# Padding the ragged weights of layer 3's last run to 128 by 128, and turning layer 1's column numbers from a 128-wide buffer

## The chip, the core and the metric

The kernel runs on one core of a Trainium2 chip. The number that counts is the device time of one execution in microseconds (us). A core has five engines, each with an instruction stream of its own that it works off in order: PE multiplies matrices (a load of the stationary operand, PEld, and then a matmul that streams the moving operand), DVE does elementwise work and reductions, ACT applies functions, POOL is a general engine for elementwise work, and SP only starts transfers here. They meet through semaphores alone: an instruction that waits holds up everything behind it on its engine.

## The reference, cut to what matters

Four graph layers over one dense 2708 x 2708 adjacency matrix that is mostly zero, with 128 features. Each layer is `x = x + layer(relu(layernorm(x)), adj)`:

```python
# layer 0: a weighted mean over the graph
x = x + (adj.T @ h) / adj.sum(axis=0)[:, None]
# layer 1: a message for every edge, then an update
messages = gelu(s[:, None, :] + d[None, :, :] + msg_b)
aggregated = einsum('ijd,ij->id', messages, adj)
...
# layer 2: agg = adj @ h, then a gated recurrent cell
# layer 3: graph attention with two heads
for i in range(2):
    e = leaky_relu(s_src[:, None] + s_dst[None, :])
    e = where((adj > 0) | eye(n), e, NEG)
    att = layernorm(softmax(e, axis=1) @ h_i + x)
    h_next = h_next + elu(att @ ff1_w[i].T) / 2
```

What matters for the change is layer 3's product `softmax(e) @ h_i`, and in layer 1 the list of column numbers of the nonzero entries. Numbers are fp32, but for small integers and split values, which are bf16.

## The kernel before

2708 rows are 21 tiles of 128 (`P`) and one of 20 (`TAIL`), so `NT` is 22; `size(t)` is the height of tile t, `span(t, k)` the first column and the number of columns of k tiles, here up to the end of the matrix. The last tile is ragged wherever it appears: as 20 rows of a stationary operand (its contraction), or as 20 columns of it.

**Layer 3, weights.** Each nonzero of the attention matrix is, up to factors that cancel, `max(row, lift) * mask`: a row of numbers that is the same for all partitions, a number for each partition, and the 0/1 mask as uint8. `weigh(run, unit, pool)` (L923) makes a tile `wt` of these on DVE in one instruction. A *run* is a group of consecutive target tiles, and `RUNS = ((0, 3), (3, 8), (11, 8), (19, 3))`: the last one holds tiles 19, 20 and the ragged 21, so it is 276 columns wide. A *unit* is one source tile j and one head k, 44 of them to a run.

**Layer 3, products.** `products` (L955) walks over the units. It asks for the weights of unit u, and then multiplies with those of unit u - 3 (u - 2 in the first run): for each of the run's target tiles q, 128 columns of `wt` are the stationary operand and `hv[:, j, k, :]`, 129 wide (128 features and the sum of weights), is the moving one. As the operands are fp32, one such product stands in the trace as two loads and two matmuls. In the last run the third target tile has 20 columns; in the last two units of every run `wt` and `hv` have 20 rows. A pool `l3w` of five buffers holds the weights, so DVE can be at most five units ahead of PE.

**What goes on beside.** The results of a run gather in PSUM banks. `evacuate` copies them out to `res` at the start of the next run (on ACT and DVE), and `close` then turns two target tiles at a time into output: scaling and a layer norm on DVE (L1018, L118 to L131, with a power on POOL, L121), a rescale on ACT (L137), transposes (L1029) and a product (L1038) on PE, an exponential linear unit on ACT and POOL, two sums on DVE (L1055, L1056) and a store. These steps are put between the products by a clock counted in estimated us (`spend`, `advance`, `follow`): the order on each engine is written out by hand (`tc.manual_schedule()`), and no engine reorders it. The last run's results are read straight from PSUM (`in_place`).

**Layer 1.** For each row tile t, `place` makes on DVE the list of the nonzero values and of their column numbers (`where`, 128 x 22 bf16, one column for each block of 124 matrix columns). `pass_on(t)` (L552) transposes `where` on PE, copies it out on ACT, stores it to DRAM and loads it back broadcast to all partitions; `columns` makes one-hot matrices from it. PE's main work here is `combine` (L612, L616) and `gather` (L637). `period(t)` puts the steps of one tile in order by hand; there are 22 tiles.

**Layer 2 and what it leaves.** `aggregate` loads pieces of the transposed matrix (`a`, five source tiles by 512 columns, three buffers) on SP's queue, writes `mask` from them, four fifths on DVE (L1086) and one fifth on POOL (L1089), and multiplies (L1094). A buffer is free for the next load when DVE, POOL and PE have all read it. Layer 3's lasting tiles (`hv`, `lift`, `row`, `score`, `mask`) are made just ahead of layer 2, in space that layer 1 has left; `score`'s last tile is set to zero there on POOL (L887), since its rows 20 to 127 are read later.

Of the kernel before, what the change touches and what calls it, by code (L numbers as in the profile page):

```python
# [20 lines left out]
F32 = mybir.dt.float32  # L21
BF16 = mybir.dt.bfloat16
AF = mybir.ActivationFunctionType
ALU = mybir.AluOpType
AX = mybir.AxisListType
# [5 lines left out]
P = 128  # L31
N = 2708
D = 128
NT = (N + P - 1) // P
# [10 lines left out]
NB = (N + JB - 1) // JB  # L45
S = 8
E = P
# [4 lines left out]
def size(t):  # L52
    return min(P, N - t * P)
# [7 lines left out]
def listed_layers(ctx: ExitStack, tc: tile.TileContext, x, adj, w, out, flag):  # L61
    nc = tc.nc
# [84 lines left out]
    def span(t, k):  # L147

        return t * P, min(k * P, N - t * P)
# [29 lines left out]
    ident_h = keep.tile([P, P], BF16, name="ident_h")  # L179
# [25 lines left out]
    with tc.tile_pool(name="l0c", bufs=1) as fix:  # L205
# [33 lines left out]
        with (  # L239
# [76 lines left out]
            with tc.manual_schedule():  # L316
# [4 lines left out]
                for gi, (g0, gk) in enumerate(GROUPS):  # L321
# [11 lines left out]
                    for j in range(NT):  # L333
# [6 lines left out]
                        n = g0 + j // 5  # L340
# [54 lines left out]
    with (  # L395
# [25 lines left out]
            nc.gpsimd.tensor_tensor(dst[2], rest, dst[1], ALU.subtract)  # L421

        state = {}

        def count_rows(t):
            some = work.tile([P, NB, S], BF16, name="some")
            nc.vector.tensor_scalar(some, val[:, t, :, :], 0.0, None, ALU.is_gt)
            with nc.allow_low_precision("counts up to 8"):
                nc.vector.reduce_sum(rows_n[:, t, :], some, AX.X)

        def compare(dst, numbers, op):

            nc.vector.tensor_tensor(  # L433
                dst.rearrange("p b (x r) -> p b x r", r=R),
                count_h.rearrange("p (x r) -> p x r", r=R).unsqueeze(1).to_broadcast([P, NB, P // R, R]),
                numbers.unsqueeze(2).to_broadcast([P, NB, P // R, R]),
                op,
            )
# [60 lines left out]
        def place(t):  # L499

            st = state[t]
            lead = st["lead"]
            slot = work.tile([P, NB], F32, name="slot")
            nc.vector.tensor_scalar(slot, lead[:, :, R], part, -1.0, ALU.subtract, ALU.mult)
            hot = once.tile([P, NB, S], F32, name="hot")
            nc.vector.tensor_tensor(
                hot,
                count[:, 0:S].unsqueeze(1).to_broadcast([P, NB, S]),
                slot.unsqueeze(2).to_broadcast([P, NB, S]),
                ALU.is_equal,  # L510
            )
            picked = once.tile([P, NB, 4, S], F32, name="picked")
            for half, y in enumerate(st.pop("ys")):
                bs = slice(half * HB, (half + 1) * HB)
                nc.vector.tensor_tensor(
                    picked[:, bs, :, :],
                    y[:, :, 0 : 4 * S].rearrange("p b (q s) -> p b q s", s=S),
                    hot[:, bs, :].unsqueeze(2).to_broadcast([P, HB, 4, S]),
                    ALU.mult,
                )  # L520
            value = work.tile([P, NB], F32, name="value")
            where = work.tile([P, NB], BF16, name="where")
            with nc.allow_low_precision("column numbers"):
                nc.vector.tensor_reduce(where, picked[:, :, 3, :], AX.X, ALU.max)
            nc.vector.reduce_sum(value, picked[:, :, 0:3, :], AX.XY)
            mine = work.tile([P, NB, P], BF16, name="mine")
            compare(mine, lead[:, :, 0:R], ALU.is_equal)
            st["value"], st["where"], st["mine"] = value, where, mine
# [19 lines left out]
        def pass_on(t):  # L548

            st = state[t]  # L550
            p = rpool.tile([P, 2 * CH], BF16, tag="r", name="p_w")
            nc.tensor.transpose(p[0:NB, 0:E], st.pop("where"), ident_h)  # L552
            turned = work.tile([NB, E], BF16, name="where_T")
            nc.scalar.copy(turned, p[0:NB, 0:E])
            passed = wdram.tile([NB, E], BF16, name="passed")
            nc.sync.dma_start(passed, turned)
            st["spread"] = once.tile([P, NB, E], BF16, name="spread")
            nc.sync.dma_start(
                st["spread"].rearrange("p b e -> p (b e)"), passed.rearrange("b e -> (b e)").partition_broadcast(P)
            )  # L560
# [148 lines left out]
        def period(t, between=()):  # L709
# [5 lines left out]
            for k in range(GB):  # L715
# [32 lines left out]
                if k == 3 and b:  # L748
                    place(t + 2)
# [132 lines left out]
    mask = l3.tile([P, NT, N], U8, name="mask")  # L882
    hv = l3.tile([P, NT, 2, D + 1], F32, name="hv")
    lift = l3.tile([P, NT, 2], F32, name="lift")
    row = l3.tile([P, 2, N], F32, name="row")
    score = l3.tile([P, NT, 4], F32, name="score")
    nc.gpsimd.memset(score[:, NT - 1, :], 0.0)  # L887
    ident_8 = l3.tile([P, P], U8, name="ident_8")
    nc.vector.tensor_copy(ident_8, ident)
    PIECE = 5  # L890
    RUNS = ((0, 3), (3, 8), (11, 8), (19, 3))
    MOST = 8
# [9 lines left out]
    def spend(units):  # L902
        clock[0] += units

    def advance():

        for f in list(following):
            while f[1] <= clock[0]:
                wait = next(f[0], None)
                if wait is None:  # L910
                    following.remove(f)
                    break
                f[1] = clock[0] + wait

    ready = set()

    def weigh(run, unit, pool):

        c, n = span(*run)
        j, k = divmod(unit, 2)  # L920
        kj = size(j)
        wt = pool.tile([P, n], F32, name="wt")
        nc.vector.scalar_tensor_tensor(  # L923
            wt[0:kj, :], row[0:kj, k, c : c + n], lift[0:kj, j, k : k + 1], mask[0:kj, j, c : c + n],
            op0=ALU.max, op1=ALU.mult,
        )
        return wt

    def products(run, numbers, pool, ahead, before=None):

        banks = None
        wts = []
        units = 2 * NT
        touched = set()
        for u in range(units + ahead):
            if u < units:
                while u // 2 not in ready:
                    spend(0.5)
                    advance()
                wts.append(weigh(run, u, pool))  # L940
            v = u - ahead
            if v < 0:
                continue
            if v == 0:
                if before:
                    before()
                banks = banks_of(run, numbers)
            r0, rn = run
            j, k = divmod(v, 2)
            kj = size(j)  # L950
            wt = wts[v]
            for q in range(rn):
                m = size(r0 + q)
                s = k * rn + q
                nc.tensor.matmul(  # L955
                    banks[s // 3][0:m, s % 3, :], wt[0:kj, q * P : q * P + m], hv[0:kj, j, k, :],
                    start=(v < 2 and s // 3 not in touched), stop=(j == NT - 1), skip_group_check=True,
                )
                touched.add(s // 3)
            spend(0.29 * rn)  # L960
            advance()
        return banks

    def banks_of(run, numbers):
        return [
            accs.tile([P, CH], F32, tag=f"acc{b}", name="att")[:, 0 : 3 * (D + 1)].rearrange("p (s d) -> p s d", s=3)
            for b in numbers[0 : (2 * run[1] + 2) // 3]
        ]
# [15 lines left out]
    def evacuate(run, banks):  # L984

        r0, rn = run
        res = out_pool.tile([P, 2 * MOST, D + 1], F32, name="res")
        inv3 = out_pool.tile([P, 2 * MOST], F32, name="inv3")
        tails = (rn - 1, 2 * rn - 1) if size(r0 + rn - 1) < P else ()
        for s in tails:  # L990
            nc.gpsimd.memset(res[:, s, :], 1.0)
        s = 0
        while s < 2 * rn:
            k = min(3 - s % 3, 2 * rn - s)
            m = P
            if s in tails:
                k, m = 1, TAIL
            elif s + k - 1 in tails:
                k -= 1
            copy = nc.vector.tensor_copy if s // 3 % 3 == 2 else nc.scalar.copy  # L1000
            copy(res[0:m, s : s + k, :], banks[s // 3][0:m, s % 3 : s % 3 + k, :])
            s += k
        nc.vector.reciprocal(inv3[:, 0 : 2 * rn], res[:, 0 : 2 * rn, D])
        return [res[:, s, :] for s in range(2 * rn)], inv3, True
# [64 lines left out]
    with (  # L1069
# [140 lines left out]
        for g, (t0, k0) in enumerate(GROUPS):  # L1210
# [6 lines left out]
            advance()  # L1217
        last = RUNS[0]
        banks = products(last, (0, 1), vpool, 2)

    out_pool = ctx.enter_context(tc.tile_pool(name="l3o", bufs=2))
# [5 lines left out]
    over = out_pool.tile([P, 1], F32, name="over3")  # L1227
    nc.vector.reduce_sum(over, wide, AX.XY)
    nc.vector.tensor_tensor(flag, flag, over, ALU.add)

    with tc.tile_pool(name="l3w", bufs=5) as wpool, tc.manual_schedule():
        for run, numbers in zip(RUNS[1:], ((2, 3, 4, 5, 0, 1), (2, 3, 4, 5, 0, 1), (2, 3))):
# [4 lines left out]
            banks = products(run, numbers, wpool, 3, work_off)  # L1237
# [467 lines left out]
```

## Time and profile before

| | us |
|---|---|
| median of 3 runs (1072.81 to 1073.6) | 1073.51 |
| span of the profiled execution, first to last instruction | 1069.6 |
| what lies around it, against the median | 3.9 |

| engine | busy, us | share of the span |
|---|---|---|
| PE, matmuls | 950.0 | 89% |
| DVE | 824.4 | 77% |
| PE, weight loads | 754.1 | 71% |
| ACT | 515.4 | 48% |
| POOL | 398.7 | 37% |

The stages follow each other: layer 0 to about 240 us, layer 1 to 615 us, layer 2 to about 785 us, layer 3's runs to 1047 us (the last run's products begin at 998 us), and the closing of the last run to the end. Of the page, the part on slices shows this as rows of 40 digits: PE is at 9 in nearly all slices of layers 1 to 3 and drops to 3 in the last one.

A line of a group of instructions reads: source line, engine, operation, output<-inputs, shapes (partitions x elements), count | busy us, mean ns of one | idle time of the engine ahead of them and what ended it. For PE `128*20` means 128 rows and 20 columns of weights. A line of a timeline reads: start, duration, the same, and in brackets the idle time ahead of it. Matmuls overlap: what counts is from start to start of one to the next, not their duration.

### The profile page before, as it was taken

How to read it: one execution, taken by the hardware profiler on the slowest of the kernel's cores; microseconds unless marked ns; L12 is line 12 of the kernel's file. 1: busy time of each engine (PE TensorE's matmuls, PEld its weight loads, DVE VectorE, ACT ScalarE, POOL GpSimd, SP SyncE). 2: the span in 40 equal slices, each digit the busy share in tenths (PEclk: the TensorE clock that was granted, in tenths of full speed). 3: DMA queues.
4: the chain of work that ended last, by engine and by line, in shares of the span. 5: the costliest groups of instructions: out<-in, count | busy, mean ns of one | idle time of the engine just before them, and what ended most of it. 6: DMA issues, size and time to landing. Idle time of an engine off the chain costs nothing. (4 is left out here: it accounts for less than half of the span.)

```text
span 1069.6 us, 21992 instructions
## 1 busy us (share of the span) xinstructions
PE 950.0 (89%) x7950; PEld 754.1 (71%) x7950; DVE 824.4 (77%) x2853; ACT 515.4 (48%) x1428; POOL 398.7 (37%) x476
## 2 busy tenths in 40 slices
PE   5798889934799999999999979999978999999993
PEld 2454445433799999899899934444578999999772
DVE  7999999768577798787878265666578977997673
ACT  7777777634766666666666522433321200320142
POOL 3311112022776656666766163343410300430132
PEclk9999999766799999999999979999989999999996
DMA  9888996221233433322221075566300000000000
GB/s 365 315 303 316 316 342 243 78 65 46 88 109 106 124 95 106 106 91 83 97 96 57 28 256 186 185 225 216 91 22 26 9 1 1 6 15 1 2 15 14
DMA packets 60625, 129.67 MB, mean 121 GB/s; under 512 B 11160, under 2 KB 23828, under 8 KB 57798
## 3 DMA queue, kind: packets, MB, share of 16 engines
q1 hardware_dynamic: 58690, 125.38, 34.2%
q10 hardware_dynamic: 1816, 2.80, 0.8%
q8 instruction: 64, 1.05, 0.4%
q14 instruction: 55, 0.45, 0.1%
HBM read 81.55 MB, written 30.87 MB: 105 GB/s over the span
## 5 line engine op out<-in xcount | busy, mean ns | idle before, releaser
L955 PE MATMUL att<-hv,wt 128*128 128x129 f32 (+2 forms) x1936 | 243.8, 283 | 8.7 <-DVE wt L923 8.7
L955 PEld LDWEIGHTS att<-hv,wt 128*128 128x128 f32 (+2 forms) x1936 | 224.7, 192 | 25.8 <-DVE wt L923 10.1
L923 DVE SCALAR_TENSOR_TENSOR wt<-row,lift,mask 128x1024 f32<-128x1024 f32 (+5 forms) x176 | 160.3, 939 | 34.9 <-PE att L955 34.8
L536 POOL TENSOR_SCALAR put<-mine,value 128x128 f32<-128x128 bf16 x176 | 149.8, 867 | 70.3 <-DVE mine L433 67.9
L612 PE MATMUL p_m<-s,sel 128*128 128x128 bf16 x1452 | 161.6, 220 | 5.4 <-ACT g L624 5.4
L616 PE MATMUL p_m<-d,cols 124*128 124x128 bf16 (+1 forms) x1452 | 161.7, 220 | 1.4 <-DVE cols L566 1.3
L121 POOL TENSOR_TENSOR n_r<-n_r,minus_half 128x4 f32<-128x4 f32 (+1 forms) x31 | 46.1, 1486 | 286.5 <-DVE n_r L120 280.9
L637 PE MATMUL agg<-put,g 128*128 128x128 f32 (+1 forms) x968 | 135.9, 281 | 0.0
L297 PE MATMUL acc<-a,hs 128*128 128x512 f32 (+2 forms) x264 | 124.4, 574 | 10.8 <-ACT hs L137 10.8
L309 PEld LDWEIGHTS p_T<-ident,a 128*128 128x128 f32 x484 | 60.1, 144 | 88.3 <-issue 40.3
L637 PEld LDWEIGHTS agg<-put,g 128*128 128x128 f32 x968 | 118.2, 192 | 0.0
L1094 PE MATMUL p_agg<-a,hs 128*128 128x512 f32 (+2 forms) x264 | 109.3, 556 | 7.3 <-DMA a<-adjT 7.2
L612 PEld LDWEIGHTS <-sel 128*128 128x128 bf16 x1452 | 104.3, 98 | 10.8 <-issue 7.0
L285 DVE FIND_INDEX8 col<-val,a 128x8 uint16<-128x124 f32 (+1 forms) x400 | 108.1, 285 | 0.0
L309 PE MATMUL p_T<-ident,a 128*128 128x128 f32 x484 | 82.3, 289 | 26.2 <-ACT aT L313 19.4
L624 ACT ACTIVATE g<-p_m 128x512 f32<-128x512 f32 x132 | 73.1, 554 | 63.8 <-PE p_m L616 63.8
L616 PEld LDWEIGHTS <-cols 124*128 124x128 bf16 (+1 forms) x1452 | 102.5, 98 | 1.9 <-DVE cols L566 1.9
L544 ACT ACTIVATE put<-mine,value 128x128 f32<-128x128 bf16 x308 | 100.5, 391 | 0.0
L283 DVE MAX8 val<-a 128x8 f32<-128x124 f32 (+1 forms) x400 | 92.8, 276 | 2.5 <-DMA a<-in_adj 2.5
L313 ACT ACTIVATE aT<-p_T 128x512 f32<-128x512 f32 (+2 forms) x132 | 71.1, 541 | 47.9 <-ACT aT L313 32.7
L1094 PEld LDWEIGHTS p_agg<-a,hs 128*128 128x128 f32 (+1 forms) x264 | 47.5, 194 | 55.8 <-issue 54.2
L297 PEld LDWEIGHTS acc<-a,hs 128*128 128x128 f32 (+1 forms) x264 | 44.7, 202 | 25.9 <-issue 14.8
(252 smaller groups left out, 1418.7 us busy)
## 6 DMA issues: line engine op xcount, KB each, us to landing
a<-in_adj SPq DMA_DIRECT2D x21, 1354.0 KB
adjT<-aT SPq DMA_DIRECT2D x105, 256.0 KB
a<-adjT SPq DMA_DIRECT2D x20, 1280.0 KB
spread<-passed SPq DMA_DIRECT2D x22, 704.0 KB
later<-sel SPq DMA_DIRECT2D x22, 616.0 KB
row<-own_d ACTq DMA_DIRECT2D x10, 256.0 KB
later<-sel SPq DMA_DIRECT2D x22, 82.5 KB
adjT<-aT SPq DMA_DIRECT2D x21, 74.0 KB
```

The costliest lines, as they stand in the source:

```text
L283: nc.vector.max(val[:, n, b, :], block(b))
L285: nc.vector.max_index(col[:, n, b, :], val[:, n, b, :], block(b))
L297: nc.tensor.matmul(accs[ci][:, 0:cw], h[0:m, n, :], sets[n // 4][0:m, n % 4, c : c + cw], start=(n == 0), stop=(n == NT - 1),)
L309: nc.tensor.transpose(p[0:k, q * P : q * P + m], sets[gi][0:m, q, j * P : j * P + k], ident[0:m, 0:m])
L536: nc.gpsimd.tensor_scalar(st["put", 0][:, b, :], st["mine"][:, b, :], st["value"][:, b : b + 1], None, ALU.mult)
L544: nc.scalar.activation(st["put", 1][:, b - HP, :], st["mine"][:, b, :], AF.Identity, scale=st["value"][:, b : b + 1])
L612: nc.tensor.matmul(p[:, b - b0, :], st["sel"][:, b, :], s3[:, q, t % 2, :], start=(q == 0), stop=False)
L616: nc.tensor.matmul(p[:, b - b0, :], st["cols"][0:kb, b, :], d3[0:kb, b, q, :], start=False, stop=(q == 2))
L637: nc.tensor.matmul(agg, g[:, b - 4 * k, :], put, start=(b == 0), stop=False)
L923: nc.vector.scalar_tensor_tensor(wt[0:kj, :], row[0:kj, k, c : c + n], lift[0:kj, j, k : k + 1], mask[0:kj, j, c : c + n], op0=ALU.max, op ...
L955: nc.tensor.matmul(banks[s // 3][0:m, s % 3, :], wt[0:kj, q * P : q * P + m], hv[0:kj, j, k, :], start=(v < 2 and s // 3 not in touched), ...
L1094: nc.tensor.matmul(pa[:, 0:n], h[0:k, j, :], a[0:k, j - j0, 0:n], start=(j == 0), stop=(j == NT - 1))
```

## The change

Layer 3's last run writes its weights to five buffers of its own, `padded`, 384 columns wide, which are set to zero once ahead of the second run; columns 276 to 383 stay zero. All products of all runs then take 128 columns and 128 rows of weights and write 128 rows of PSUM. For the ragged source tile the last tiles of `hv`, `lift` and `mask` are set to zero on POOL ahead of layer 2, so rows 20 to 127 of the weights and of `hv` are zero. `res` has one buffer instead of two. In layer 1, `where` becomes one of two lasting 128 x 128 buffers (set to zero once), of which the first 22 columns are written and all 128 are transposed.

```diff
         state = {}
+        wheres = [fix.tile([P, P], BF16, name=f"where{q}") for q in range(2)]
+        for q in range(2):
+            nc.gpsimd.memset(wheres[q], 0.0)
...
-            where = work.tile([P, NB], BF16, name="where")
+            where = wheres[t % 2]
             with nc.allow_low_precision("column numbers"):
-                nc.vector.tensor_reduce(where, picked[:, :, 3, :], AX.X, ALU.max)
+                nc.vector.tensor_reduce(where[:, 0:NB], picked[:, :, 3, :], AX.X, ALU.max)
...
-            nc.tensor.transpose(p[0:NB, 0:E], st.pop("where"), ident_h)
+            nc.tensor.transpose(p[:, 0:E], st.pop("where"), ident_h)
...
     nc.gpsimd.memset(score[:, NT - 1, :], 0.0)
+    nc.gpsimd.memset(hv[:, NT - 1, :, :], 0.0)
+    nc.gpsimd.memset(lift[:, NT - 1, :], 0.0)
+    nc.gpsimd.memset(mask[:, NT - 1, :], 0)
...
+    padded = []
+
     def weigh(run, unit, pool):
 
         c, n = span(*run)
         j, k = divmod(unit, 2)
-        kj = size(j)
-        wt = pool.tile([P, n], F32, name="wt")
+        wt = pool.tile([P, n], F32, name="wt") if n == run[1] * P else padded[unit % len(padded)]
         nc.vector.scalar_tensor_tensor(
-            wt[0:kj, :], row[0:kj, k, c : c + n], lift[0:kj, j, k : k + 1], mask[0:kj, j, c : c + n],
+            wt[:, 0:n], row[:, k, c : c + n], lift[:, j, k : k + 1], mask[:, j, c : c + n],
             op0=ALU.max, op1=ALU.mult,
         )
         return wt
...
             j, k = divmod(v, 2)
-            kj = size(j)
             wt = wts[v]
             for q in range(rn):
-                m = size(r0 + q)
                 s = k * rn + q
                 nc.tensor.matmul(
-                    banks[s // 3][0:m, s % 3, :], wt[0:kj, q * P : q * P + m], hv[0:kj, j, k, :],
+                    banks[s // 3][:, s % 3, :], wt[:, q * P : (q + 1) * P], hv[:, j, k, :],
                     start=(v < 2 and s // 3 not in touched), stop=(j == NT - 1), skip_group_check=True,
                 )
...
-        res = out_pool.tile([P, 2 * MOST, D + 1], F32, name="res")
+        res = out_pool.tile([P, 2 * MOST, D + 1], F32, bufs=1, name="res")
...
+
+    for q in range(5):
+        padded.append(out_pool.tile([P, RUNS[-1][1] * P], F32, tag=f"padded{q}", bufs=1, name=f"padded{q}"))
+        nc.gpsimd.memset(padded[q], 0.0)
```

## The prediction, made before the changed kernel was run

> **What bounds the kernel now.** I read the page's slices first: PE is at 9 tenths through layers 1 to 3, DVE between 7 and 9, DMA idle after layer 2. The chain that ended last holds only the last microsecond, so it carries nothing; stages have to be read one by one. Next the busy times of two stretches, one in the middle of an eight-tile run and one in the last run (columns: length, then busy time and count of PE, PEld, DVE, ACT, POOL, granted clock, DMA):
>
> ```profile
> 960.00:980.00 20.00, 20.00 (x182) 20.00 (x181) 14.70 (x13) 0.00 (x0) 0.00 (x0) 1.00 0.00 1
> 1003.00:1009.00 6.00, 6.00 (x38) 3.98 (x38) 3.72 (x12) 1.65 (x4) 0.00 (x0) 1.00 0.00 1
> ```
>
> PE is full in both, at the same clock, but in the first it starts a matmul every 0.110 us (20/182), in the second every 0.158. The timeline of weight loads shows why (three units of the last run):
>
> ```profile
> 1003.99 0.76 PEld L955 LDWEIGHTS att<-hv,wt 128*128 128x128 f32 x6 [0.21 <-issue]
> 1004.96 0.76 PEld L955 LDWEIGHTS att<-hv,wt 128*128 128x128 f32 x6 [0.21 <-issue]
> 1005.93 0.76 PEld L955 LDWEIGHTS att<-hv,wt 128*128 128x128 f32 x6 [0.21 <-DVE n_r L128]
> ```
>
> A unit of six matmuls takes 0.97 us; six at the other rate would take 0.66. The 0.21 of idle on the load side recurs at every return to full width. To the nanosecond, the matmul starts within a unit are 0.11 apart between full ones, but 0.205 into the 20-column pair, 0.124 within it and 0.204 out of it. So crossing from one shape of weights to another costs about 0.09 each way. The same stands in layer 1 (PE's timeline):
>
> ```profile
> 337.01 0.72 PE L637 MATMUL agg<-put,g 128*128 128x128 f32 x5
> 337.67 0.23 PE L552 MATMUL p_w<-ident_h,where 128*22 128x128 bf16 x1
> 337.82 0.34 PE L612 MATMUL p_m<-s,sel 128*128 128x128 bf16 x3
> ```
>
> The last L637 starts at 337.46 and L552 0.205 later, where L637 to a full-width L612 elsewhere takes 0.111; L552 to L612 is 0.157, where L612 to L612 takes 0.056. Now DVE in the last run, by groups over 999 to 1042:
>
> ```profile
> L923 DVE SCALAR_TENSOR_TENSOR wt<-row,lift,mask 128x276 f32<-128x276 f32 x37 | 18.4, 526 | 5.4 <-PE att L955 5.4
> L923 DVE SCALAR_TENSOR_TENSOR wt<-row,lift,mask 20x276 f32<-20x276 f32 x2 | 1.0, 497 | 1.0 <-PE att L955 1.0
> ```
>
> PE sets the pace there, but DVE waits for it only 6.4 us in 43. That is the next bound. Then the entry to layer 2, where the change adds work on POOL:
>
> ```profile
> 629.37 0.10 POOL L887 MEMSET score<- 128x4 f32 x1 [0.57 <-DVE xs L694]
> 629.45 7.15 POOL L1089 TENSOR_SCALAR mask<-a 128x512 uint8<-128x512 f32 x3
> ...
> 632.02 3.48 SPq L1082 DMA_DIRECT2D a<-adjT  x2
> ...
> 637.86 1.10 PE L1094 MATMUL p_agg<-a,hs 128*128 128x512 f32 x2 [1.11 <-DMA a<-adjT]
> ```
>
> The first of POOL's three masks ends at 631.99 and SP issues the fourth load at 632.02; PE runs dry and waits 1.11 us for that load. This path has no slack. Last, the granted clock around the 20-row units that end a run (they start at 903.7 and 993.9):
>
> ```profile
> 902.83:906.24 3.41, 3.41 (x31) 3.29 (x30) 2.21 (x3) 0.96 (x2) 0.00 (x0) 1.00 0.02 5
> 906.24:909.65 3.41, 3.41 (x17) 3.18 (x16) 2.21 (x5) 0.96 (x2) 0.00 (x0) 0.50 0.00 0
> 994.99:998.40 3.41, 3.41 (x30) 3.17 (x29) 1.50 (x5) 1.81 (x4) 0.00 (x0) 1.00 0.02 5
> 998.40:1001.81 3.41, 3.41 (x13) 2.16 (x14) 3.24 (x16) 0.00 (x0) 0.11 (x1) 0.50 0.00 0
> ```
>
> After each such stretch the clock is halved, though PE was never idle.
>
> **What the skill says.** "TensorEngine Tiling (Array Packing)", Key Properties: changing the tiling mode drains the engine. The trace agrees, with 0.09 us each way, and a return to 128 columns costs as much as leaving it. "TensorE: Matmul & The Clock Gate", What's actually happening: the clock is halved by default and freed by activity, judged in windows of some 3.4 us. The trace's steps are 3.41 us, and here a window filled with 20-row matmuls counted as inactive. "VectorE: DVE Perf Modes", Zero memsets can be issued as uint32: a memset takes one cycle per element whatever the type. POOL's two large ones agree (2359 ns for 2708 fp32, 2444 for 2816 bf16: 0.87 ns each); no uint8 one is in the trace. "SBUF — State Buffer", Who interferes with whom: DVE in a two-port mode and POOL lock each other out. POOL's first two masks took 2.55 and 3.18 us beside DVE's masks, 1.48 alone.
>
> **The change part by part.** In the program built from it, the order on every engine is the old one but for ten more memsets on POOL; no DMA is added.
>
> *Last run.* On PE alone, 44 units x (0.97 - 0.66) = 13.6 us go. The loads of the third tile grow from 98 to 196 ns, but in the full runs loads of 196 ns lie under matmuls started every 0.110 us: nothing. DVE's instruction still writes 276 columns, and 20 or 128 rows take the same (497 against 526): nothing. But DVE cannot give 13.6. Its four closings each put about 3 us of other work in one block between the weights; the last block ends at 1031.3. Of its 6.4 us of waits 4.9 lie before that, so undisturbed it ends at 1026.4, with PE empty by then. From there PE has 12 units x 0.66 = 7.9, plus two groups of products and one of transposes (20 matmuls x 0.11 = 2.2), plus 0.5 for the first weight: 1037.0, where it ended at 1046.9. That is 9.9; I take 9.3, leaving 0.6 for waits between ACT's rescale (1.65 us for four) and the transposes. Bounds: 6.4, DVE's waits alone, and 13.6.
>
> *Run ends.* The 20-row units cost one crossing in and one out in each of three runs: 6 x 0.09 = 0.55 saved.
>
> *Clock.* If padded rows count as activity, the half clock at 906.24 to 913.06 goes. Run 1's last matmuls (to 908.17) gain 0.97 and DVE's waits after it (0.13 and 0.22) 0.35, sum 1.3; after that DVE is full until 961 and nothing more is won. The one at 824.3 falls where PE waits for DVE anyway, the one at 998.4 is in the sum above. Bounds 0 and 1.3; I take 1.3.
>
> *Layer 1.* 22 transposes x (0.205 - 0.111 + 0.157 - 0.056) = 4.3 us on PE. The list of waits has PE waiting 8.9 us in 12 places (for ACT's g, DVE's sel and cols). A gain ahead of such a wait is lost unless the chain waited for starts on PE itself; DVE waiting 19.7 us for PE's p_s says that many do. Bounds 2.0 (10 places without a wait) and 4.3; I take 3.0. ACT copies 22 rows as before.
>
> *Entry to layer 2.* Ahead of POOL's first mask come `hv` (258 elements, 0.3), `lift` (0.05) and `mask` (2708 at 0.87 = 2.36): 2.7 us. Queued behind are the masks, behind those SP's fourth load, behind that PE and all that follows. Lower bound: without any lock the first mask ends at 629.45 + 2.7 + 1.48 = 633.6, 1.7 late. Upper bound: all the locking of the three masks (7.15 - 3 x 1.48 = 2.7) falls ahead of it: 636.3, 4.3 late. I take 3.2. The fifth load has 4 us of slack and moves too. POOL's power for the last tile's norm, behind the masks, comes later, but PE needs its result only at 642.
>
> *Nothing.* The five `padded` memsets (384 x 0.87 = 0.33 each, 1.7) wait for the last chunk's transposes at 792.5, and stand ahead of a power at 794.33 whose result DVE takes at 798.6: 3.4 us of cover; without it 1.7. The two `where` memsets (0.15 each) fall in POOL's 9.65 us of idle ahead of 237.2. `res` is rewritten at 996, long after run 1's closings read it. The tail after the last product stays.
>
> Sum: -9.3 - 0.55 - 1.3 - 3.0 + 3.2 = -10.95. Against its own execution 1069.6 becomes 1058.65; with the 3.9 around it, 1062.6 against the median of 1073.51.
>
> **Rivals.** *PE's rate all the way (0.12):* DVE keeps up, all 13.6 are won, layer 1 gives 4.3, the entry costs 1.7, the rest as above: -18.05, 1055.5. DVE's 6.4 us speaks against it. *DVE's slack only (0.17):* 6.4 in the last run, 2.0 in layer 1, no clock gain, the entry at 4.3: -4.65, 1068.9. For it: closings on DVE are stretched by POOL (a weight of 967 ns at 1035.7). *Loads set the pace (0.07), slower:* in the last run full loads can't hide, and a unit takes 6 x 0.196 = 1.18 us: 44 x 0.21 = 9.2 lost, with the rest -1.65: +7.6, 1081.1. It makes the kernel slower by itself once a unit exceeds 1.01 us; the full runs, where such loads do hide, speak against it. *No crossing cost (0.03):* the 0.09 comes of something else that stays, as the order of banks; nothing is won and the entry costs 3.2: 1076.7. L637 into full L612 at 0.111 speaks against.
>
> **How the numbers follow.** The sum's case has 0.61, with 1059 to 1066.5 from its bounds. To hold 8 in 10 the range takes in the slack case and the near half of the fast one: 1056.5 to 1069.5; the two slow cases, 0.10, stay out. A change under 0.2% (2.1 us) can't be told from none: slower has 0.09 of the two slow ones, same 0.03 from between, faster 0.88.
>
> **What would show it.** Unit starts in the last run 0.66 apart where PE isn't waiting; DVE without waits for PE between 1003 and 1026, and PE waiting for `wt` instead; the products' end near 1037 less what came before; clock 1.00 after each run's end; L552 0.11 after L637; PE's wait for the fourth load near 4.3 us. The forecast is wrong if loads spread to 0.19 apart, or if the uint8 memset takes far more than 2.4 us: at the 2.9 ns per element of POOL's mask it would be 7.8, and the gain would halve.

## The result and the profile after

| | before | after |
|---|---|---|
| median, us | 1073.16 (4 runs, 1071.84 to 1073.6) | 1064.1 (4 runs, 1062.2 to 1066.37) |
| ratio to before, 95% interval | | 0.9915 (0.9891 to 0.9939) |
| span of the profiled execution, us | 1069.6 | 1064.6 |
| PE matmuls busy, us | 950.0 | 929.8 |
| DVE busy, us | 824.4 | 826.0 |
| POOL busy, us | 398.7 | 402.1 |

The change makes the kernel 9.1 us faster; 10.95 were forecast. The profiled execution of the changed kernel is the slowest of its four (1066.37), so its span has fallen by only 5.0. A later comparison of the same kernel gave 1063.96 against 1071.72, ratio 0.9935 (0.9918 to 0.9953). The gain is therefore 7 to 9 us.

The busy times of stretches (columns as before) of the changed kernel: the middle of an eight-tile run, the last run, and twice 3.4 us at and after the source tile that used to have 20 rows, whose two units run from 908.3 to 911.8 here:

```profile
962.00:982.00 20.00, 20.00 (x181) 20.00 (x181) 15.20 (x13) 0.00 (x0) 0.00 (x0) 1.00 0.00 1
1006.00:1012.00 6.00, 6.00 (x57) 6.00 (x56) 5.76 (x23) 2.43 (x5) 0.00 (x0) 1.00 0.00 0
...
907.80:911.20 3.40, 3.40 (x32) 3.40 (x32) 2.39 (x3) 0.98 (x3) 0.00 (x0) 1.00 0.02 5
911.20:914.60 3.40, 3.40 (x33) 3.40 (x32) 3.27 (x9) 0.94 (x2) 0.00 (x0) 1.00 0.00 0
```

PE starts 57 matmuls in 6 us of the last run where it started 38: one every 0.11 us or so, as in the full runs. Full loads do not spread. DVE has gone from 3.72 to 5.76 of 6. The clock stays at 1.00 where it was halved. The groups over the last run, 1001 to 1042, put the wait on the other side:

```profile
L960 PE MATMUL att<-hv,padded 128*128 128x129 f32 x259 | 32.3, 278 | 4.5 <-DVE padded L930 4.5
...
L930 DVE SCALAR_TENSOR_TENSOR padded<-row,lift,mask 128x276 f32<-128x276 f32 x40 | 18.3, 514 | 0.0
```

DVE's weights never wait for PE; PE's products wait for DVE's weights. In layer 1, PE's timeline at the same tile as before:

```profile
336.38 1.11 PE L640 MATMUL agg<-put,g 128*128 128x128 f32 x8
337.32 0.22 PE L555 MATMUL p_w<-ident_h,where 128*128 128x128 bf16 x1
337.38 0.33 PE L615 MATMUL p_m<-s,sel 128*128 128x128 bf16 x3
```

The transpose is followed 0.06 us later by the next matmul, not 0.157. Last, the entry to layer 2, on POOL, SP and PE (timeline; the first line is PE's before the change):

```profile
637.86 6.44 PE L1094 MATMUL p_agg<-a,hs 128*128 128x512 f32 x14 [1.11 <-DMA a<-adjT]
...
627.18 2.35 POOL L893 MEMSET mask<- 128x2708 uint8 x1
629.51 5.54 POOL L1094 TENSOR_SCALAR mask<-a 128x512 uint8<-128x512 f32 x2
...
632.64 2.76 SPq L1087 DMA_DIRECT2D a<-adjT  x2
...
617.98 14.81 PE L1099 MATMUL p_agg<-a,hs 128*128 128x512 f32 x30 [6.16 <-DMA a<-adjT]
638.58 8.08 PE L1099 MATMUL p_agg<-a,hs 128*128 128x512 f32 x14 [5.79 <-DMA a<-adjT]
```

PE waits 5.79 us for the fourth load instead of 1.11, and the 14 matmuls behind it take 8.08 us instead of 6.44.

The whole is easiest seen by stages of PE's timeline. Layer 1 is from the first transpose of `where` to the last; layer 2 from the first `p_agg` product to the last; the full runs from the last `p_hv` product (the end of layer 2's work) to the last run's first product; the last run from its first product to its last. All are counted from start to start, in us, of one execution each; the names are those of the experiments below:

| | layer 1 | layer 2 | full runs | last run |
|---|---|---|---|---|
| before | 340.88 | 153.05 | 182.69 | 49.07 |
| after | 338.35 | 160.93 | 180.39 | 41.28 |
| after, once more | 338.41 | 159.06 | 180.40 | 41.31 |
| `where` alone | 338.41 | 153.27 | 181.02 | 47.60 |
| columns alone | 340.92 | 152.79 | 182.47 | 41.83 |
| rows alone | 340.93 | 158.78 | 182.06 | 47.51 |
| zeroes later | 338.39 | 154.17 | 180.41 | 41.32 |
| ragged apart | 338.38 | 152.92 | 181.72 | 41.29 |
| PE kept busy, 5 | 338.38 | 157.83 | 180.43 | 41.31 |
| weights ahead | 338.50 | 158.87 | 179.00 | 41.73 |

Outside these stages executions differ by themselves: the first transpose comes between 242.79 and 246.34 us in kernels that share the same layer 0.

### The profile page after: what moved, and what is told of

It reads as the page before. It is cut to its first block, busy times and chain, and to the rows that moved or that the text cites. A ratio compares the mean times of both kernels' runs of the same rounds, so it can differ in the third digit from the quotient of the medians.

```text
span 1064.6 us, 22002 instructions
## 1 busy us (share of the span) xinstructions
PE 929.8 (87%) x7950; PEld 749.6 (70%) x7950; DVE 826.0 (78%) x2853; ACT 515.7 (48%) x1428; POOL 402.1 (38%) x486
## 5 line engine op out<-in xcount | busy, mean ns | idle before, releaser
L960 PE MATMUL att<-hv,wt 128*128 128x129 f32 x1672 | 194.4, 277 | 8.7 <-DVE wt L930 8.7
L960 PEld LDWEIGHTS att<-hv,wt 128*128 128x128 f32 x1672 | 190.9, 193 | 11.7 <-DVE wt L930 8.6
L930 DVE SCALAR_TENSOR_TENSOR wt<-row,lift,mask 128x1024 f32<-128x1024 f32 (+1 forms) x132 | 138.7, 1081 | 23.3 <-PE att L960 23.3
L285 DVE FIND_INDEX8 col<-val,a 128x8 uint16<-128x124 f32 (+1 forms) x400 | 104.8, 269 | 0.0
L283 DVE MAX8 val<-a 128x8 f32<-128x124 f32 (+1 forms) x400 | 90.1, 261 | 1.9 <-DMA a<-in_adj 1.9
```

Source lines behind the costliest of these rows:

```text
L283: nc.vector.max(val[:, n, b, :], block(b))
L285: nc.vector.max_index(col[:, n, b, :], val[:, n, b, :], block(b))
L930: nc.vector.scalar_tensor_tensor(wt[:, 0:n], row[:, k, c : c + n], lift[:, j, k : k + 1], mask[:, j, c : c + n], op0=ALU.max, op1=ALU.mult,)
L960: nc.tensor.matmul(banks[s // 3][:, s % 3, :], wt[:, q * P : (q + 1) * P], hv[:, j, k, :], start=(v < 2 and s // 3 not in touched), stop=( ...
```

## Experiments: the parts alone

**Layer 1's part alone**, on the kernel before: the `where` lines of the diff and nothing else.

> The kernel before, with layer 1's part of the change alone (where in lasting 128-wide buffers, transposed whole). If PE's crossings are what is won and about a third of them lie ahead of waits for other engines: 3.0 us less than before (1070.2 against 1073.2), and the first matmul after a transpose follows it by 0.06 us less than before on either side. If all 22 count: 4.3 less. If the waits take it back: 2.0 less or nothing.

Ratio 0.9977 (0.9962 to 0.9992), 2.5 us (medians 1067.66 against 1071.43). Layer 1 takes 338.41 us instead of 340.88, as in the whole change: its gain is that of these lines. It is less than the 4.3 of all 22 transposes. That the rest is lost to PE's waits for other engines, as supposed, is not shown.

**The columns alone**: `padded` for the last run, 128 columns, the source tile's 20 rows kept.

```diff
+        wt = pool.tile([P, n], F32, name="wt") if n == run[1] * P else padded[unit % len(padded)]
...
-                    banks[s // 3][0:m, s % 3, :], wt[0:kj, q * P : q * P + m], hv[0:kj, j, k, :],
+                    banks[s // 3][:, s % 3, :], wt[0:kj, q * P : (q + 1) * P], hv[0:kj, j, k, :],
```

> The kernel before, with the five padded buffers of the last run alone: its third tile takes 128 columns, but the ragged source tile keeps its 20 rows everywhere, and nothing is added on POOL ahead of layer 2. If DVE is what bounds the last run once PE's crossings are gone: the run's products take about 41.3 us from first to last as in the changed kernel (49.1 before), PE and not DVE waits in it, and the time is some 7.8 us under before: 1065.4. The 20-row units at the ends of runs 1 and 2 stay, so the halved clock after them (906 to 913) should stay as well; if it goes, it was not the rows that brought it. If PE's own rate decides: 13.6 less, 1059.6.

Ratio 0.9938 (0.9916 to 0.9959), 6.6 us (medians 1063.85 against 1071.43); the last run takes 41.83 us. So the last run's gain is that of the columns. The halved clock stayed, at 822, 907 and 996, behind each run's end.

**The rows alone**: the three settings to zero and 128 rows everywhere, the last run's 20 columns kept.

```diff
+    nc.gpsimd.memset(hv[:, NT - 1, :, :], 0.0)
+    nc.gpsimd.memset(lift[:, NT - 1, :], 0.0)
+    nc.gpsimd.memset(mask[:, NT - 1, :], 0)
...
-                    banks[s // 3][0:m, s % 3, :], wt[0:kj, q * P : q * P + m], hv[0:kj, j, k, :],
+                    banks[s // 3][0:m, s % 3, :], wt[:, q * P : q * P + m], hv[:, j, k, :],
```

> The kernel before, with the rows alone: hv, lift and mask of the last tile set to zero on POOL ahead of layer 2, 128 rows in every product, but the last run keeps its 20 columns. If zero rows count as activity for the clock: no halved clock at 824, 906 and 998. Sum: 5.3 to 7.9 more at the entry to layer 2 (as the changed kernel shows there), 0.55 less for the run ends, 1.3 to 2 less for the clock: about 4 us slower than before, 1077. If the entry costs only the 3.2 that was forecast: 1 to 2 slower, 1075. If the entry's cost is an accident of one execution: no slower than before.

Ratio 1.0012 (0.9997 to 1.0026): 1.3 us slower, and the interval takes in no change. No window behind a run's end is halved. Layer 2 costs 5.7 us more than before, with this line in PE's timeline:

```profile
642.25 8.32 PE L1095 MATMUL p_agg<-a,hs 128*128 128x512 f32 x14 [5.70 <-DMA a<-adjT]
```

So the rows by themselves bring nothing that pays for the entry. By stages this execution is 3.5 us slower (+5.7 in layer 2, -0.6 and -1.6 in the runs, the last one since its beginning no longer lies in a halved window), near the 4 expected; the medians show 1.3.

By the ratios the three parts come to -2.5, -6.6 and +1.3 us, together -7.8: the gain of the whole, 7 to 9.

## Experiments: the entry to layer 2

**The zeroes later**, on the changed kernel.

```diff
-    nc.gpsimd.memset(hv[:, NT - 1, :, :], 0.0)
-    nc.gpsimd.memset(lift[:, NT - 1, :], 0.0)
-    nc.gpsimd.memset(mask[:, NT - 1, :], 0)
...
                 m = size(j0 + most)
+                if m < P:
+                    if c == 0:
+                        nc.gpsimd.memset(hv[:, NT - 1, :, :], 0.0)
+                        nc.gpsimd.memset(lift[:, NT - 1, :], 0.0)
+                    nc.gpsimd.memset(mask[:, NT - 1, c : c + n], 0)
```

> The changed kernel, with the three settings to zero moved: hv and lift, and the mask in pieces of 512 columns, each on POOL just ahead of the 20-row mask of its chunk. If the 2.35 us memset ahead of POOL's first mask is what makes the fourth load late: the load is issued 3 us earlier, PE waits for it 1 to 2 us instead of 5.8, the clock isn't halved there, and the time is 5.3 us under the changed kernel's 1064.1: 1058.8. If the lock between DVE's and POOL's masks decides when that load starts, whatever stands ahead: PE still waits over 4 us and the time stays above 1062.

1058.64 us, ratio to before 0.989 (0.9868 to 0.9913). The same three engines:

```profile
625.30 7.15 POOL L1096 TENSOR_SCALAR mask<-a 128x512 uint8<-128x512 f32 x3
...
635.20 0.53 POOL L1095 MEMSET mask<- 128x512 uint8 x1
...
627.87 3.48 SPq L1084 DMA_DIRECT2D a<-adjT  x2
...
633.54 6.44 PE L1101 MATMUL p_agg<-a,hs 128*128 128x512 f32 x14 [1.85 <-DMA a<-adjT]
```

POOL's three masks take 7.15 us again and the load starts 2.6 us after the first of them began, as before the change; the wait is 1.85, the 14 matmuls take 6.44. The memsets ahead of the masks were what delayed the load, and the lock between the masks was not. This version beats both kernels; its interval lies below the 0.9918 to 0.9953 of the change's second comparison, if barely, and overlaps with that of the first (0.9891 to 0.9939).

**PE kept busy in the wait**, on the changed kernel: does the halved clock after the wait come of PE's idleness?

```diff
+            if t0 == 0 and j0 == 3 * PIECE:
+                idle = accs.tile([P, CH], F32, tag="acc5", name="idle")
+                for q in range(11):
+                    nc.tensor.matmul(
+                        idle, h[:, q, :], h[:, 0:4, :].rearrange("p t d -> p (t d)"), start=True, stop=True
+                    )
```

> The changed kernel, with 11 products into a PSUM bank that nothing reads put ahead of the products that need layer 2's fourth load: 4.7 us of work in PE's 5.8 us of waiting. If the halved clock after that wait (635 to 642) comes of PE's idleness and is a part of what the entry costs: no halved clock there, the 14 products behind the wait take 6.4 us instead of 8.1, and the time is 1.6 less, 1062.5. If not: no change in the 8.1. Either way the load itself lands as late as before.

1067.32 us, ratio 0.9952 (0.9935 to 0.9969): 3.4 us above the change in the same comparison, where the two intervals just touch. The clock was not halved and the 14 matmuls took 6.36 us, but the filling was mis-sized: such a product is two matmuls of 0.43 us, not one, and the 22 ended 5.3 us after the load. Five products instead (`range(5)`):

> As the experiment that kept PE busy, with 5 products instead of 11: a product of 512 fp32 columns is two matmuls of 0.43 us, so 11 of them were 9.5 us and reached 5.3 us past the load; 5 are 4.3 us and end before it. If the clock's part of the entry is real: no halved clock behind the wait, the 14 products 6.4 us instead of 8.1, the fourth load as late as in the changed kernel, layer 2's products 157.4 us from first to last instead of 159.1, and some 1.6 us under the 1063.96 of the change. If one idle window of PE's is enough in any case: the 8.1 stay.

1062.43 us, ratio 0.9915 (0.9895 to 0.9935). PE's timeline:

```profile
632.43 4.45 PE L1100 MATMUL idle<-hs 128*128 128x512 f32 x10
638.30 6.44 PE L1105 MATMUL p_agg<-a,hs 128*128 128x512 f32 x14 [1.41 <-DMA a<-adjT]
```

The busy times of the windows behind the wait, twice the changed kernel and then this run (columns as before, the clock third from the end):

```profile
635.06:638.47 3.41, 0.00 (x0) 0.00 (x0) 1.22 (x5) 0.88 (x2) 2.15 (x2) 0.50 1.03 389
638.47:641.89 3.42, 3.31 (x4) 1.52 (x5) 2.69 (x6) 0.00 (x0) 3.37 (x2) 0.50 0.97 326
...
638.74:642.15 3.41, 3.41 (x9) 1.52 (x8) 2.14 (x6) 0.00 (x0) 3.41 (x2) 1.00 0.97 366
```

With the load just as late, 6.44 in place of 8.08 to 8.72: 1.6 to 2.3 us of the entry is clock, lost because PE stood idle. The gain in the median, 1.5 us, is within the intervals; the 6.44 is what shows it. The wait need not be longer than a window for this. The version with the zeroes later was profiled a second time as the base of the weights further ahead, below, with the load as early as in its first profile (11.9 us after layer 2's first product, 11.8 there):

```profile
633.62 8.13 PE L1101 MATMUL p_agg<-a,hs 128*128 128x512 f32 x14 [2.44 <-DMA a<-adjT]
```

A wait of 2.44 us, which lay in one window of 3.41 (630.53 to 633.95), was followed by half the clock; the 1.85 of the first profile, which lay in one window too, were not. So the later zeroes take away the load's delay each time, but not always the halved clock.

**The change once more**, for a wait of 0.94 us at 733.6 that only layer 2 of the changed kernel's first profile had.

> The changed kernel once more, beside the version with ragged units apart. If the wait of 0.94 us at 733.6 and the halved clock behind it were that execution's own: no such wait, layer 2's products (p_agg, from first to last) take about 158.8 us instead of 160.9, and the median is 1063 to 1065. If they belong to the change: they are there again.

1063.96 us; no such wait, layer 2 159.06 us. That wait came from a load that took 7.6 us where the same one took 6.8 before, and it belongs to single executions: it was there again in the experiments with half the weights (1.23 us) and with the weights ahead (1.07 us), and not in the rows alone.

## Experiments: the last run

**Half the weights**, on the changed kernel.

```diff
+        if n < run[1] * P and unit > 5 and unit % 2:
+            return wt
```

> The changed kernel, but in the last run every second weight from unit 7 on is left out on DVE (19 of 44 instructions; PE multiplies with what the buffer held), so part of the attention is not computed. If DVE bounds the last run: DVE is relieved of 19 x 0.42 = 8 us, PE goes on at 0.67 a unit, and the run's products take 32 to 34 us from first to last instead of 41.3; the time falls by 7 to 9, to about 1056. If PE, or the rescale on ACT ahead of the transposes, sets the pace: under 3 us less.

1060.95 us, ratio 0.9899 (0.9879 to 0.9919); the last run takes 37.09 us. Groups over it:

```profile
L962 PE MATMUL att<-hv,padded 128*128 128x129 f32 x261 | 31.2, 276 | 1.8 <-DVE padded L932 1.8
...
L932 DVE SCALAR_TENSOR_TENSOR padded<-row,lift,mask 128x276 f32<-128x276 f32 x21 | 11.5, 571 | 1.4 <-PE att L962 1.4
```

Less work on DVE and nothing else is changed, and the run is 4.2 us shorter: DVE is the bound. It is less than the 7 to 9 expected, as the estimate left out that PE has four closings' products of its own to do: 48 matmuls x 0.11 = 5.3 us beside 43 x 0.67 = 28.8. Together with two remaining waits (1.8) that is 36 of the 37.

**Weights further ahead**, on the version with the zeroes later.

```diff
+            if run == RUNS[-1]:
+                for q in range(5):
+                    two = wpool.tile([P, 8 * P], F32, name="wt")[:, 0 : 6 * P].rearrange("p (s n) -> p s n", s=2)
+                    nc.gpsimd.memset(two[:, :, span(*run)[1] :], 0.0)
+                    padded.extend([two[:, 0, :], two[:, 1, :]])
-            banks = products(run, numbers, wpool, 3, work_off)
+            banks = products(run, numbers, wpool, 8 if run == RUNS[-1] else 3, work_off)
```

> The version with the zeroes moved, and the last run's weights two to each of the five buffers of the pool l3w: ten deep, DVE eight units ahead of PE instead of three. DVE idles 5.4 us at the end of the run before (it has five units ready and waits for PE's last products before it may copy the results out); three weights of 0.42 us go into that. If DVE bounds the whole last run: 1.3 us less in the last run (40.0 instead of 41.3) and not more, since every weight still costs DVE its 0.42; PE's waits move to the run's end. If it was the depth of the buffers, so that PE starved only during DVE's blocks of closing work: PE's seven waits, 5.2 us, mostly go, and the run takes 36 to 37.

1059.41 us, ratio 0.9882 (0.9867 to 0.9897), not to be told from the version it was made from (1058.64). Groups over 996 to 1036.5:

```profile
L957 PE MATMUL att<-hv,wt 128*128 128x129 f32 x254 | 29.8, 275 | 0.0
...
L927 DVE SCALAR_TENSOR_TENSOR wt<-row,lift,mask 128x276 f32<-128x276 f32 x35 | 16.2, 518 | 0.0
...
L1031 PE MATMUL p_aT<-ident,att_s 128*128 128x128 f32 x16 | 5.2, 328 | 3.7 <-ACT att_s L137 3.0
```

No product waits for a weight any more, and still nothing is won but what DVE did earlier: from the last `p_hv` product to the last product 220.73 us instead of 221.73. PE now waits 3.0 us for ACT's rescale, which waits for the norm on DVE. With DVE full from end to end, deeper buffers only choose which of its results PE waits for.

## Experiment: the clock at the end of a run

The columns alone had three halved windows behind the runs' ends, `where` alone had none there, with the same 20-row units. What differs is where the windows fall. Groups of PE in the window that holds most of the 20-row products, for the kernel before (902.83 to 906.24):

```profile
L955 PE MATMUL att<-hv,wt 20*128 20x129 f32 x22 | 2.8, 276 | 0.0
L955 PE MATMUL att<-hv,wt 128*128 128x129 f32 x9 | 1.2, 275 | 0.0
```

and for `where` alone (986.19 to 989.60), whose next window kept the clock of 1.00:

```profile
L958 PE MATMUL att<-hv,wt 20*128 20x129 f32 x20 | 2.5, 276 | 0.0
L958 PE MATMUL att<-hv,wt 128*128 128x129 f32 x11 | 1.4, 275 | 0.0
```

If the share of full rows decides, spreading the 20-row products is enough:

```diff
+        order = list(range(units))
+        if before:
+            order = order[0:14] + [42] + order[14:28] + [43] + order[28:42]
...
-            j, k = divmod(v, 2)
+            j, k = divmod(order[v], 2)
```

> Layer 1's part and the padded columns, but no zero rows at all: the two units of the ragged source tile keep 20 rows, and in the last three runs they are taken out of the end and put at places 14 and 29 of 44, so that no 3.41 us hold more than 16 products of 20 rows out of some 31. If a window is judged by how much of it is work on full rows (22 of 28 with 20 rows were followed by half the clock, 20 of 29 were not): no halved clock at any of these places, four crossings a run instead of two, nothing added at the entry to layer 2, and a time near that of the version with the zeroes moved: 1059.5. If any stretch of 20-row products halves the clock: six halved windows, and 4 to 8 us more than that.

1060.51 us, ratio 0.9898 (0.9882 to 0.9915). The fullest window of run 1, by groups, and the clock in it and in the next:

```profile
L962 PE MATMUL att<-hv,wt 128*128 128x129 f32 x17 | 2.1, 275 | 0.0
L962 PE MATMUL att<-hv,wt 20*128 20x129 f32 x15 | 1.9, 277 | 0.0
```

```profile
876.61:880.03 3.42, 3.42 (x32) 3.30 (x31) 2.57 (x2) 0.00 (x0) 0.00 (x0) 1.00 0.00 0
880.03:883.44 3.41, 3.41 (x32) 3.29 (x31) 2.32 (x2) 0.00 (x0) 0.00 (x0) 1.00 0.00 0
```

None of the six places is followed by half the clock. The two halved windows of this execution, at 822 and 934.6, stand behind the end of the first run, which was left as it was, and behind a window in which PE started 10 matmuls of full rows where some 31 fit, since it waited for ACT's rescale. Without a zero row, and with nothing at the entry, this version too is faster than the change: 3.5 us in the same comparison.

## Why the prediction was right, and where it was off

The total was right (1062.6 forecast, 1064.1 measured), though two terms were too good, by 1.5 and 2.8 us. By its steps, with the change's second profile, where the wait at 733.6 does not stand in the way:

- *Last run, -9.3 forecast, -7.8 measured.* The mechanism was right: unit starts are 0.67 apart where PE does not wait, PE waits and DVE does not. The term that was mis-sized most is the one after DVE's last closing block: "From there PE has 12 units x 0.66". In the change's first profile, that block ends at 1029.64, 29.4 us after the run's first product, where 28.7 were forecast. But DVE still owes weights, sums and the rest of a norm, and its last weight ends at 1038.54, 8.9 us later; the last product starts 3.0 us after that, so that 11.9 us stand where 10.6 were forecast. DVE's rate, not PE's, holds to the end: from the first closing to the last weight 43.1 us before, 37.2 after, which is nearly the bound "DVE's waits alone" (6.4). The rest is the shorter tail on PE behind the last weight, 4.9 to 3.0 us. Half the weights and the weights ahead confirm it. PE's rate all the way would have been about 34 us for the run (28.8 + 5.3, as above; an estimate).
- *Run ends and clock, -1.85 forecast, -2.3 measured* (182.69 to 180.4 in the full runs). Zero rows count as activity: in none of the eight profiles with zero rows is the clock halved behind a run's end. But the halved windows before were not a fixed cost of 20 rows: they depended on how the windows fell. `where` alone kept its 20 rows, lost no clock behind a run's end and took 181.02: so some 0.6 us are crossings, and the other 1.7 are clock that this one execution of the kernel before had lost. The prediction also read the price of a crossing too low. The starts of single matmuls before the change show 0.205 into the 20 rows and 0.200 out of them, but each time 0.214 to the start after that, where 0.11 is usual: about 0.2 us a crossing. In the last run's units, too, the first gap between full products is 0.214 and not the 0.11 that it names, so the way back costs nearly twice the way into the 20 columns. The same 0.214 stands behind PE's waits for `padded` in the changed kernel's last run. The last run's term took whole units (0.97) and is not touched; of the run ends' six crossings, 1.2 us at this price, 0.6 came out of the kernel's time.
- *Layer 1, -3.0 forecast, -2.5 measured*, inside its bounds, alone and in the whole.
- *Entry to layer 2, +3.2 forecast, +6.0 measured*: the largest miss, outside the bound of 4.3. The uint8 memset took 2354 ns for 2708 elements, as forecast, and so did the load's delay come out: from POOL's memset of `score` to the fourth load 2.65 us pass in every profile without the zeroes ahead of the masks, and 5.84 to 5.87 in every one with them, 3.2 more. What was left out is the second effect of the wait: PE, idle for over 5 us, has its clock halved, 1.6 to 2.3 us more in the next 14 matmuls. The prediction counted clock where 20-row units ran and not where its own step made PE idle. The rest is no cost: layer 2's first product comes 0.9 us sooner after layer 1's last transpose (34.41 us instead of 35.29), so that the stage begins sooner and PE waits longer for the same load. Counted from that transpose, the 14 matmuls end 5.4 us later than before (4.8 in the first profile), and 3.1 later with PE kept busy by five products.
- *Nothing.* The memsets of `padded` and `where`, and the one buffer of `res`, show in no stage; none of them was tried alone.

Of the rivals, "loads set the pace" and "no crossing cost" are refuted by 57 matmuls in 6 us. "DVE's slack only" has come nearest in the last run and at the entry, and was wrong about the clock and layer 1.

By stages the change's second profile is 6.3 us shorter than before's (-2.5, +6.0, -2.3, -7.8, and +0.3 behind the last product). The spans of these two executions differ by 9.1. Of the other 2.8, 2.0 lie ahead of layer 1's first transpose (244.81 and 242.86), which differs by up to 3.5 us in any case, and 0.9 between layer 1's last transpose and layer 2's first product. There PE's clock is halved in both, but from 29.1 us after the transpose instead of 27.0; why the window falls later is not shown. The prediction named neither. By the steps it named, it was 10.95 against 6.3, so it is in part luck that the total came as close as 1.5 us.

## What to carry to other kernels

A ragged operand costs PE a change of shape at every crossing, and padding it with zeroes is worth the larger matmul, but the gain is only the waits of the next engine: count that engine's work to the very end, not to its last big block. Put preparations behind the first instruction that a load waits for, and in pieces where they are used; moving three memsets here brought 1064 us down to 1059, where the whole change had won 7 to 9. Where a step makes PE idle for microseconds, add the slower clock behind the wait to its price, even if the wait is shorter than a window (2.44 us were enough here).

## What the runs showed of the hardware

- A window of the clock seems to be judged by rows at work, not by matmuls. Windows of 31 products, of which 22 or 25 had 20 rows, were followed by half the clock, though PE was never idle; with 20, 19 or 15 of 31 to 32 they were not. The limit lies between 20 and 22. The Trainium skill, "TensorE: Matmul & The Clock Gate", What's actually happening, says that windows run freely and do not start with the kernel. The traces agree: the same kernel's second profile has them elsewhere. So the same code keeps or loses clock from one execution to the next, here 1 to 2 us a time.
- Idle time and few rows count in one measure. Take each matmul at its pace at full clock (129 fp32 columns start 0.110 us apart, so 0.85 ns a column, and 128 bf16 columns 0.056), times its rows as a share of 128, and add up what falls into a window of 3.41 us. Over the twelve profiles, 3274 windows ran at full clock. All 129 in which this sum is below 0.36 of the window were followed by half the clock, and none of the 3127 above 0.40; of the 18 between, 7 were. The fullest 20-row window of run 1 before has 0.33, the one of `where` alone 0.39, the window of the changed kernel's wait for the fourth load 0.29, and the one with the wait of 2.44 us 0.24.
- A memset on POOL, which reads nothing, held up DVE's first mask: 3.29 us beside it, 1.20 before, and the mask ended 1.08 us after the memset did. The Trainium skill, "SBUF — State Buffer", Who interferes with whom, has POOL and DVE in a two-port mode lock each other out. The trace fits this; that the mask runs in such a mode, no trace shows. The fourth load did not wait for it: in the changed kernel's first profile DVE's mask ended at 630.61, POOL's first at 632.62, and the load started at 632.64.
